# Two FP4 layers and the linear attention between them, chained: FP4's last and first turns placed among the linear tiles

## The chip, the cores and the metric

The kernel runs on one core of a Trainium2 chip. The core has four compute engines that each work through a queue of their own in order: TensorE (PE, with its weight loads shown apart as PEld), VectorE (DVE), ScalarE (ACT) and GpSimd (POOL), and a fifth, SyncE (SP), that issues DMAs. The metric is the device time of one execution in microseconds; the number compared is the median of several executions.

## The reference

Six layers work on `x` of 4 x 1024 tokens by 256 channels, each on the layer norm of `x`, each added back to it:

```
x = x + 0.5 * moe(norm(x))            # router over 4 experts, GELU
x = x + softmax_attention(norm(x))    # 16 heads, causal
x = x + 0.5 * moe(norm(x))
x = x + 0.5 * fp4_ffn(norm(x))        # first FP4 layer
x = x + linear_attention(norm(x))     # causal, 16 heads of 16
x = x + 0.5 * fp4_ffn(norm(x))        # second FP4 layer
```

The change concerns the last three. The FP4 layer is `fp4_linear(silu(gate) * up, w_down)` with `gate` and `up` each an `fp4_linear` of the input (256 to 704). `fp4_linear` first rounds both operands to a grid of sixteen signed values: per block of 16 elements `scale = max(max|x| / 6, 1e-12)`, then `q = nearest grid value of x / scale, times scale`. Both the layer's inputs and its hidden values (704 a token) go through it.

The linear attention takes `q`, `k`, `v` from one product of 256 to 768, passes `q` and `k` through `square(gamma * normalized + beta)`, and computes for each token `q . cumsum(k v^T)`, divided by `q . cumsum(k)`, and a last product of 256 to 256.

## The kernel before, in words

`x` lies in SBUF as eight tiles `x0` to `x7` of 128 partitions by 4 x 256 and stays there. Tokens are taken in 32 tiles of 128.

**An FP4 layer** (`fp4_phase`, L1122) runs sixteen turns, one for each pair of tiles, and two more that drain. All four engines have their order written out by hand here (`tc.manual_schedule`). One turn `p` works on several pairs at once:

- `fp4_statistics(p+3)` and `fp4_deviation(p+3)`: mean and variance on DVE (L1226, L1227), the root on ACT (L1232);
- `fp4_offset(p+2)`, `fp4_inputs(p+2)`: two tiny DVE operations (L1237, L1239) and the normalized input `xn` on ACT (L1247);
- `fp4_inputs_scale(p+2)`, `fp4_inputs_rounded(p+2)`: block maxima `xam`, their reciprocals, `xv = xn / scale`, the exponent `xm` (DVE, L1042 to L1051), `fp4_least` on ACT (L1057), two rounding operations on DVE (L1061, L1062) and `xq` on POOL (L1261);
- `fp4_inputs_turned(p+1)`: transposes of `xq` on PE (L1285), a copy on ACT;
- `fp4_products(p, j)` for both tiles `j` of the pair: eight matmul rows into `pairA` (gate) and eight into `pairB` (up) (L1298), then SiLU on ACT (L1307); `fp4_gated(p, j)` multiplies on DVE (L1312) into `h`;
- `fp4_scale` on both tiles' `h` at once: `ham`, `hrs`, `hv`, `hm` (the same lines L1042 to L1051, 128 x 1408), with the residual of `p-1` between the reciprocal and `hv`;
- in the next turn `fp4_hidden_begin` (two halves of `fp4_least` on ACT), `fp4_hidden_rounded(p-1, j)` (L1061, L1062 on DVE, `hq` on POOL, L1276), `fp4_hidden_turned(p-1, j)` (transposes L1319, copies L1320), `fp4_down` (L1327, into the one bank `acc`) and `fp4_residual` (L1334), which adds into `x`; in the last layer it also sends the tile out by a DMA on SP.

DVE's order at the start of a turn is: statistics of `p+3`, rounding of `p-1` tile 0, offset of `p+2`, rounding of `p-1` tile 1, gate of `p` tile 0.

**The linear attention** (`linear_phase`, L1342) works by single tiles. Only PE's order is written out; DVE, ACT and POOL are ordered by the framework's scheduler, which may also move such instructions ahead into the FP4 layer before. For a tile `n` there are: `linear_products(n)` (L1394; bias on DVE L1402, statistics L1407, root L1410 on ACT, normalized `qk` L1420, gamma and beta on POOL L1424, L1425, square on ACT into `ker`, L1427), `linear_turn` (transposes of `ker`, L1437, and four copies on ACT), `linear_scores` (L1456 into `pairA` and `pairB`, the causal mask on DVE into `sc`, L1465, the running state on PE, DVE and POOL, L1475 to L1498), `linear_values` (L1507 into `acc`), `linear_out` (L1522 to L1528), `linear_back` and `linear_project` (L1540, L1549, residual L1551). Step `n` runs scores of `n`, products of `n+2`, projection of `n-3`, turn of `n+1`, values of `n`, back of `n-2`, out of `n-1`. Every fourth tile `linear_inputs` normalizes a block of four (L263, L264, L281 on DVE, the bias into `x` on POOL, L1383) and transposes it (L290).

PSUM is divided into `pairA` and `pairB` of two banks each, `acc`, and three banks that all other products and transposes take in rotation (`bank`).

The three phases follow each other with their own pools: the linear pool opens where the first FP4 pool lay, the second FP4 pool where the linear one lay.

Of the kernel before, what the change touches and what calls it, by code (L numbers as in the profile page):

```python
# [21 lines left out]
P = 128  # L22
# [6 lines left out]
H = 16  # L29
# [17 lines left out]
def macaron_kernel(  # L47
# [985 lines left out]
    def fp4_scale(wp, src, n, parts, tag, pinned=lambda ins: ins, between=None):  # L1033

        def temp(name, shape):
            t = wp.tile([P] + shape, F32, tag=tag + name, name=tag + name)
            return t[0:parts]

        am = temp("am", [n])
        pinned(nc.vector.tensor_reduce(am, src, AX.X, ALU.max, apply_absolute_value=True))  # L1042
        nc.vector.tensor_scalar(am, am, SIXTH, 1e-12, ALU.mult, ALU.max)
        rs = temp("rs", [n])
        nc.vector.reciprocal(rs, am)
        if between:
            between()
        v = temp("v", [n, QB])
        nc.vector.tensor_tensor(v, src, rs.unsqueeze(2).to_broadcast([parts, n, QB]), ALU.mult)  # L1049
        m = temp("m", [n, QB])  # L1050
        nc.vector.tensor_scalar(m.bitcast(U32), v.bitcast(U32), 0x7F800000, None, ALU.bitwise_and)  # L1051
        return am, v, m
# [69 lines left out]
    def fp4_phase(tag, final, fetch=None, later={}):  # L1122
        np_ = TT // 2
        with tc.tile_pool(name=f"fp4{tag}", bufs=2, reuse_waits="tile") as wp, tc.manual_schedule(
            engines={mybir.EngineType.PE, mybir.EngineType.DVE, mybir.EngineType.Activation, mybir.EngineType.Pool}
        ):
            held = {}
            for p in range(5):
                fp4_fetch(wp, p, held, fetch)
            if fetch:  # L1130
                keep_awake(50)
                for p in range(2):
                    keep_awake(4, held["back", p][:, 1, 0:P])
            for p in range(2):
                fp4_returned(p, held)
                fp4_statistics(wp, p, held)
                fp4_deviation(wp, p, held)
            if fetch:
                keep_awake(12)
            for p in range(2):  # L1140
                fp4_offset(wp, p, held)
                fp4_inputs(wp, p, held)
            if fetch:
                keep_awake(4, held["xn", 0][:, 0:P])
                keep_awake(6)
            fp4_inputs_scale(wp, 0, held)
            fp4_inputs_rounded(wp, 0, held)
            fp4_inputs_turned(wp, 0, held)
            fp4_inputs_scale(wp, 1, held)
            fp4_returned(2, held)  # L1150
            fp4_statistics(wp, 2, held)
            fp4_inputs_rounded(wp, 1, held)
            fp4_deviation(wp, 2, held)
            fp4_returned(3, held)
            for p in range(np_ + 2):
                now, before = p < np_, 1 <= p <= np_
                if p in later:
                    later[p]()
                if before:
                    fp4_hidden_begin(wp, p - 1, held)  # L1160
                if p + 3 < np_:
                    fp4_statistics(wp, p + 3, held)
                if before:
                    fp4_hidden_rounded(p - 1, 0, held)
                if p + 2 < np_:
                    fp4_offset(wp, p + 2, held)
                if now:
                    fp4_products(wp, p, 0, held)
                if p + 2 < np_:
                    fp4_inputs(wp, p + 2, held)  # L1170
                if before:
                    fp4_hidden_rounded(p - 1, 1, held)
                if now:
                    fp4_gated(p, 0, held)
                if p >= 2:
                    fp4_down(wp, p - 2, 1, held)
                if p + 2 < np_:
                    fp4_inputs_scale(wp, p + 2, held)
                if p + 1 < np_:
                    fp4_inputs_turned(wp, p + 1, held)  # L1180
                if before:
                    fp4_hidden_turned(wp, p - 1, 0, held)
                if p >= 2:
                    fp4_residual(p - 2, 1, held, final)
                if p + 2 < np_:
                    fp4_inputs_rounded(wp, p + 2, held)
                if p + 4 < np_:
                    fp4_returned(p + 4, held, nc.gpsimd)
                if p + 5 < np_:
                    fp4_fetch(wp, p + 5, held, fetch)  # L1190
                if now:
                    fp4_products(wp, p, 1, held)
                    fp4_gated(p, 1, held)
                if p + 3 < np_:
                    fp4_deviation(wp, p + 3, held)
                if before:
                    fp4_down(wp, p - 1, 0, held)
                residual = (lambda: fp4_residual(p - 1, 0, held, final)) if before else None
                if now:
                    h = held.pop(("h", p))  # L1200
                    held["hs", p] = fp4_scale(
                        wp, blocks_of(h.rearrange("p j f -> p (j f)")), 2 * FI // QB, P, "h", between=residual
                    )
                elif before:
                    residual()
                if before:
                    fp4_hidden_turned(wp, p - 1, 1, held)
# [56 lines left out]
    def fp4_hidden_begin(wp, p, held):  # L1264
        am, v, m = held["hs", p]
        n = FI // QB
        for j in range(2):
            fp4_least(m[:, j * n : (j + 1) * n], P)
        held["hq", p] = wp.tile([P, 2, FI], F32, tag="hq", name="hq")

    def fp4_hidden_rounded(p, j, held):
        am, v, m = held["hs", p]
        n = FI // QB
        s = slice(j * n, (j + 1) * n)
        fp4_round(v[:, s], m[:, s])
        nc.gpsimd.tensor_tensor(  # L1276
            blocks_of(held["hq", p][:, j]), v[:, s], am[:, s].unsqueeze(2).to_broadcast([P, n, QB]), ALU.mult
# [64 lines left out]
    def linear_phase():  # L1342
        with tc.tile_pool(name="lin1", bufs=1, reuse_waits="tile") as cp, tc.tile_pool(
            name="lin", bufs=2, reuse_waits="tile"
        ) as wp, tc.manual_schedule(engines={mybir.EngineType.PE}):

            vas = [cp.tile([P, H, 32], F32, tag=f"va1{i}", name=f"va1{i}") for i in range(4)]


            state = cp.tile([P, KD, 8, 32], F32, tag="state", name="state")  # L1350
            for t in vas:
                nc.gpsimd.memset(t, 1.0)
            nc.gpsimd.memset(state, 0.0)
            held = {}

            def products(n):
                if n % TPB == 0:
                    linear_inputs(wp, n // TPB, held)
                linear_products(wp, n, vas[n % 4], held)

            for n in range(2):
                products(n)
            linear_turn(wp, 0, held)
# [278 lines left out]
```

## Time and profile before

| what | us |
|---|---|
| median of 3 runs (2437.53 to 2443.14) | 2441.64 |
| the profiled execution | 2446.59 |
| its span, first to last instruction | 2444.9 |
| first FP4 layer, its turns' `ham` from tile pair 0 to 15 | 1554.63 to 1822.40 |
| linear attention, first to last `sc` | 1863.67 to 2125.24 |
| second FP4 layer, `ham` of pair 0 to 15 | 2158.18 to 2420.45 |

Over the span PE is busy 2290.6 us (94%), DVE 1684.6 (69%), ACT 1006.1 (41%), POOL 726.1 (30%). These shares mix stages with different limits. A stage is read by asking the profile for the busy time of each engine in a stretch of the span; the granted clock is TensorE's, 1.00 being full speed. Matmuls are pipelined and their ends are modelled, so a busy PE is not PE at its peak. A steady FP4 turn takes 17.4 us, a linear tile 8.33 us (a tile with a block's transposes 9.9).

### The profile page before, as it was taken

The numbers are of one execution on the slowest core, as the hardware profiler recorded it, in microseconds if no ns is written. First come the engines' busy times: TensorE is split into PE (matmuls) and PEld (weight loads), VectorE is DVE, ScalarE is ACT, GpSimd is POOL, SyncE is SP. The second block draws the span as 40 slices with busy tenths as digits, with TensorE's granted clock in tenths as the row PEclk, the third lists the DMA queues.
The fourth block names the chain that finished last, engine by engine and source line by source line (L and its number), as shares of the span: only waits on it lengthen the run. The fifth ranks groups of instructions, "written<-read, shape, count | busy, mean of one in ns | idle before, by whom it ended". The sixth has DMA issues, their size and how long they took to land.

```text
span 2444.9 us, 37631 instructions
## 1 busy us (share of the span) xinstructions
PE 2290.6 (94%) x13607; PEld 1498.4 (61%) x13607; DVE 1684.6 (69%) x4625; ACT 1006.1 (41%) x2057; POOL 726.1 (30%) x816
## 2 busy tenths in 40 slices
PE   7999998999999999999989999899987999889998
PEld 5688884444344444444568887566765777656766
DVE  6456664766766777767533333899977888789996
ACT  3233332345544554553422332455533333345552
POOL 0344532121121111111144442455424443212221
PEclk7899999799999999998889999999998999989999
DMA  5333321011111111010043331010000000000000
GB/s 175 109 117 116 113 70 52 20 28 30 30 32 30 31 32 39 22 50 21 31 148 111 104 108 42 28 46 20 10 0 1 1 1 2 1 7 13 18 14 20
DMA packets 67554, 112.66 MB, mean 46 GB/s; under 512 B 20696, under 2 KB 47864, under 8 KB 62248
## 3 DMA queue, kind: packets, MB, share of 16 engines
q0 software_dynamic: 12192, 58.21, 7.4%
q1 hardware_dynamic: 53400, 47.44, 6.8%
q10 hardware_dynamic: 1776, 4.61, 0.6%
q8 instruction: 108, 1.77, 0.3%
q14 instruction: 78, 0.64, 0.1%
HBM read 74.11 MB, written 23.00 MB: 40 GB/s over the span
## 4 chain that ended last, share of the span: by engine, by line
PE 67%; DVE 22%; ACT 4%; issue 3%; POOL 3%; DMA 1%; another core or an unknown queue 0%; DVEq 0%; ACTq 0%; POOLq 0%; SPq 0%
PE acc L587 10%; PE bank L874 9%; PE bank L983 8%; PE acc L933 6%; PE pairA L571 6%; PE pairB L571 5%; PE bank L1394 3%; PE bank L829 3%; POOL hq L1276 2%; DVE ham L1042 2%; DVE h L1312 2%; DVE hv L1049 2%; PE bank L385 1%; PE bank L809 1%; PE bank L113 1%
## 5 line engine op out<-in xcount | busy, mean ns | idle before, releaser
L993 ACT ACTIVATE ex<-bank 128x512 f32<-128x512 f32 (+3 forms) x768 | 317.3, 497 | 352.6 <-PE bank L983 350.1
L996 POOL TENSOR_SCALAR_AFFINE_SELECT ex<-ex 128x256 f32<-128x256 f32 x256 | 103.9, 412 | 654.4 <-ACT ex L993 650.6
L874 PE MATMUL bank<-kT,qT 32*128 32x512 f32 (+3 forms) x1536 | 264.1, 551 | 6.6 <-ACT ex L993 5.5
L587 PE MATMUL acc<-wf,gT 128*128 128x256 f32 x1184 | 261.7, 379 | 0.0
L587 PEld LDWEIGHTS acc<-wf,gT 128*128 128x128 f32 x1184 | 225.0, 190 | 30.6
L593 DVE TENSOR_TENSOR y<-acc,xg 128x256 f32<-128x256 f32 x74 | 28.0, 419 | 294.9 <-issue 197.2
L983 PE MATMUL bank<-less,kT 32*128 32x512 f32 (+3 forms) x1536 | 216.0, 562 | 8.7 <-DVE mv L264 5.0
L887 DVE TENSOR_REDUCE part<-bank 128x1 f32<-128x512 f32 x256 | 160.3, 682 | 62.1 <-PE bank L874 61.6
L874 PEld LDWEIGHTS bank<-kT,qT 32*128 32x128 f32 x1536 | 120.2, 193 | 105.3 <-issue 41.8
L1327 PE MATMUL acc<-wdT,hqT 128*128 128x256 f32 x768 | 180.6, 386 | 3.4 <-DVE x L1334 2.8
L1276 POOL TENSOR_TENSOR hq<-hv,ham 128x704 f32<-128x704 f32 x64 | 106.8, 1669 | 256.5 <-DVE std L1237 154.0
L1298 PE MATMUL pairA<-wgT,xqT 128*128 128x352 f32 x512 | 169.0, 475 | 1.7 <-ACT xqT L1287 1.4
L1327 PEld LDWEIGHTS acc<-wdT,hqT 128*128 128x128 f32 x768 | 147.8, 193 | 35.6 <-ACT hqT L1320 4.0
L933 PE MATMUL acc<-ex,va 128*32 128x512 f32 (+3 forms) x1536 | 168.1, 513 | 0.1
L571 PE MATMUL pairA<-xgT,w 128*128 128x256 f32 x608 | 159.6, 385 | 8.9 <-ACT xgT L561 8.3
L983 PEld LDWEIGHTS bank<-less,kT 32*128 32x128 f32 x1536 | 81.5, 191 | 138.6 <-issue 88.4
L890 DVE CUSTOM_DVE_ANT_0 seen<-bank,mask_q,part 128x512 bf16<-128x512 f32 (+3 forms) x256 | 126.1, 547 | 54.5 <-PE bank L874 54.1
L1298 PE MATMUL pairB<-wuT,xqT 128*128 128x352 f32 x512 | 161.9, 459 | 0.0
L571 PE MATMUL pairB<-xgT,w 128*128 128x256 f32 x608 | 156.1, 379 | 0.0
L578 ACT ACTIVATE gT<-pairA,b1s 128x256 f32<-128x256 f32 x152 | 72.0, 473 | 167.7 <-PE pairA L571 163.8
L1298 PEld LDWEIGHTS pairB<-wuT,xqT 128*128 128x128 f32 x512 | 97.3, 190 | 54.3 <-issue 0.2
L890 DVE CUSTOM_DVE_ANT_0 seen<-bank,mask_q 128x512 bf16<-128x512 f32 (+3 forms) x256 | 111.2, 485 | 27.6 <-PE bank L874 24.8
(274 smaller groups left out, 4248.8 us busy)
## 6 DMA issues: line engine op xcount, KB each, us to landing
y_d<-y SPq DMA_DIRECT2D x36, 256.0 KB
xn_d<-xn SPq DMA_DIRECT2D x16, 512.0 KB
x<-in_x SPq DMA_DIRECT2D x8, 512.0 KB
kT<-qk SPq DMA_DIRECT2D x32, 128.0 KB
qT<-qk SPq DMA_DIRECT2D x32, 128.0 KB
yT<-ys SPq DMA_DIRECT2D x32, 128.0 KB
out<-x SPq DMA_DIRECT2D x32, 128.0 KB
den<-inv_d SPq DMA_DIRECT2D x112, 32.0 KB
```

The lines of the kernel that those rows point to most:

```text
L571: nc.tensor.matmul(pg[:, f, :], lhsT=w1[:, k * FF + fc * P : k * FF + (fc + 1) * P], rhs=xgT[:, k, :], start=(k == 0), stop=(k == KD - 1),)
L587: nc.tensor.matmul(po[j], lhsT=gT[fc][:, bass.ts(j, P)], rhs=wf0[:, fc, :], start=(fc == 0), stop=(fc == NF - 1))
L874: nc.tensor.matmul(ps[:, 0:cols], lhsT=qT[rows, bass.ts(qt, P)], rhs=kT[rows, c * BLK : c * BLK + cols], start=True, stop=True,)
L887: nc.vector.tensor_reduce(parts[i][:, h : h + 1], ps[:, 0:cols], AX.X, ALU.max, negate=True)
L890: nc.vector.tensor_tensor_reduce(out=seen[:, 0:cols], in0=ps[:, 0:cols], in1=mask_q[:, BLK - cols : BLK], scale=-1.0, scalar=parts[i][:, h ...
L933: nc.tensor.matmul(acc[qb][bass.ts(h, 32), c0:BLK], lhsT=va[:, kt, NG * g + h, :], rhs=exs[h // 2][:, h % 2, c0:BLK], start=(kt == 0), sto ...
L983: nc.tensor.matmul(pss[h][:, c0:BLK], lhsT=kT[rows, bass.ts(kt, P)], rhs=held["less", n, qb][rows, c0:BLK], start=True, stop=True,)
L993: nc.scalar.activation(ex[:, j, c0:BLK], pss[2 * a + j][:, c0:BLK], AF.Exp, scale=0.25)
L996: nc.gpsimd.affine_select(out=ex[:, :, c0 : c0 + P], in_=ex[:, :, c0 : c0 + P], compare_op=ALU.is_ge, fill=0.0, base=0, pattern=[[0, 2], [ ...
L1276: nc.gpsimd.tensor_tensor(blocks_of(held["hq", p][:, j]), v[:, s], am[:, s].unsqueeze(2).to_broadcast([P, n, QB]), ALU.mult)
L1298: nc.tensor.matmul(pg[:, half, 0:FIH], lhsT=held["xqT", p][:, k, j, :], rhs=w[:, k, half * FIH : (half + 1) * FIH], start=(k == 0), stop=( ...
L1327: nc.tensor.matmul(po, lhsT=hqT[:, c, :], rhs=wdT[:, c, :], start=(c == 0), stop=(c == NFI - 1))
```

## The change

The three phases become one function, `fp4_and_linear`, with all pools open at once. What it does:

1. **The order within an FP4 turn.** `fp4_phase` is split into `fp4_begin` and a generator `fp4_turn`. The statistics of `p+3` move behind the first rounding, the offset of `p+2` ahead of it; the residual of `p-1` moves from between `hrs` and `hv` to behind `hm`. In the first and the last turn (`apart`) the hidden scale is done in two halves, the first one, with its rounding, before the second gate.
2. **Linear within the last FP4 turns.** Turn 14 holds the norm of block 0, turn 15 the transposes and products of linear tile 0, and the products of tile 1 follow it; the order is written out for all engines.
3. **FP4's two draining turns** become steps behind `linear_values` of tiles 0 to 2 (1, 2 and 4 steps).
4. **The second FP4 layer's beginning** (`fp4_first`, six steps, and its turns 0 to 2, eleven steps) is placed one step a tile behind `linear_values` of tiles 20 to 31 and of the three draining steps; the last steps follow the loop. On PE they stand where they are written; on DVE, ACT and POOL `behind()` holds them back behind the last instruction that each of these queues had when the step was written.
5. **The norms** of linear blocks 1 to 7 become such steps too, at every fourth tile, two tiles ahead of their transposes; the linear `xn` takes its room from the FP4 tag `hq`, and the scores `sc` become two tiles in the rooms of `hv` and `hm` (two buffers each, as `sc` had).
6. The memsets of `va1` and `state` on POOL (L1352, L1353) move ahead of the first FP4 layer.

The diff, cut to its core:

```diff
-    def fp4_phase(tag, final, fetch=None, later={}):
...
+    def fp4_turn(wp, p, held, final, fetch=None):
         np_ = TT // 2
+        now, before = p < np_, 1 <= p <= np_
+        if before and p - 1 not in (0, np_ - 1):
+            for j in range(2):
+                fp4_hidden_least(p - 1, j, held)
+        if p + 2 < np_:
+            fp4_offset(wp, p + 2, held)
+        if before and p - 1 not in (0, np_ - 1):
+            fp4_hidden_rounded(p - 1, 0, held)
+        if p + 3 < np_:
+            fp4_statistics(wp, p + 3, held)
+        if now:
+            fp4_products(wp, p, 0, held)
+        if p + 2 < np_:
+            fp4_inputs(wp, p + 2, held)
+        if before:
+            fp4_hidden_rounded(p - 1, 1, held)
+        if now:
+            fp4_gated(p, 0, held)
+        if p >= 2:
+            fp4_down(wp, p - 2, 1, held)
+        yield
...
+        apart = p in (0, np_ - 1)
+        if now:
+            fp4_hidden_begin(wp, p, held)
+            fp4_products(wp, p, 1, held)
+        if now and apart:
+            fp4_hidden_scale(p, 0, 1, held)
+            fp4_hidden_least(p, 0, held)
+            fp4_hidden_rounded(p, 0, held)
+        if now:
+            fp4_gated(p, 1, held)
...
+        if now and not apart:
+            fp4_hidden_scale(p, 0, 2, held)
+        if before:
+            fp4_residual(p - 1, 0, held, final)
+        if now and apart:
+            fp4_hidden_scale(p, 1, 1, held)
+            fp4_hidden_least(p, 1, held)
...
+        yield
+        if before:
+            fp4_hidden_turned(wp, p - 1, 1, held)
+            yield
...
+    @contextmanager
+    def behind():
+        traced = nc.cur_bb.bb.instructions
+        with ExitStack() as stack:
+            for engine in (mybir.EngineType.DVE, mybir.EngineType.Activation, mybir.EngineType.Pool):
+                stack.enter_context(tc.issue_after(next(i for i in reversed(traced) if i.engine == engine)))
+            yield
...
+            with tc.manual_schedule(engines=all_four):
+                fp4_begin(wp, held, fetch)
+                for p in range(np_):
+                    if p in later:
+                        later[p]()
+                    turn = fp4_turn(wp, p, held, False, fetch)
+                    next(turn)
+                    if p == np_ - 2:
+                        linear_norm(wp, 0, lin)
+                    if p == np_ - 1:
+                        linear_inputs(lp, 0, lin)
+                        linear_products(lp, 0, vas[0], lin)
+                    for _ in turn:
+                        pass
+                linear_products(lp, 1, vas[1], lin)
+            ends = itertools.chain(*(fp4_turn(wp, p, held, False) for p in (np_, np_ + 1)))
             held = {}
...
+            first = itertools.chain(fp4_first(wp, held), *(fp4_turn(wp, p, held, True) for p in range(3)))
+            with tc.manual_schedule(engines={mybir.EngineType.PE}):
+                linear_phase(lp, wp, vas, state, ends, first, lin)
+            with tc.manual_schedule(engines=all_four):
+                for p in range(3, np_ + 2):
+                    for _ in fp4_turn(wp, p, held, True):
+                        pass
...
+        step_behind(ends)
+        linear_turn(wp, 0, held)
+        for n in range(TT + 3):
...
+            if n < TT:
+                linear_values(wp, n, vas[n % 4], held)
+            for _ in range((1, 2, 4)[n] if n < 3 else 0):
+                step_behind(ends)
...
+            if n >= TT - 12:
+                step_behind(first)
+            if n % TPB == 0 and n + TPB < TT:
+                with behind():
+                    linear_norm(fwp, n // TPB + 1, held)
+            if 2 <= n < TT + 2:
+                linear_back(wp, n - 2, held)
+            if 1 <= n < TT + 1:
+                linear_out(wp, n - 1, held)
...
+    def linear_norm(fwp, b, held):
+        xn = fwp.tile([P, 2, FI], F32, tag="hq", name="hq").rearrange("p j f -> p (j f)")
+        xn = xn[:, 0 : TPB * D].rearrange("p (i d) -> p i d", d=D)
         norm_block(xn, xb[b], eps5)
         nc.gpsimd.tensor_tensor(xb[b], xb[b], over_tiles(bo1), ALU.add)
+        held["xn", b] = xn
...
-        sc = wp.tile([P, 4, KD, 2, P], F32, tag="sc", name="sc")
-        for a in range(2):
+        sc = []
+        for a, tag in enumerate(("hv", "hm")):
+            room = fwp.tile([P, 2, FI // QB, QB], F32, tag=tag, name=tag).rearrange("p j n c -> p (j n c)")
+            sc.append(room[:, 0 : 8 * P].rearrange("p (r g e t) -> p r g e t", r=2, g=KD, e=2))
```

## The prediction

> **What bounds the kernel now.** I read the table by stages first, then the instructions of one steady FP4 turn, then those of one linear tile, then the two seams and the tail. All the change's work lies behind 1554 us of the span.
>
> Stages (columns: stretch, its length, then busy us of PE, PEld, DVE, ACT, POOL, granted clock, DMA share, GB/s):
>
> ```profile
> 1747.21:1786.89 39.68, 35.54 (x157) 26.00 (x157) 38.27 (x89) 24.51 (x37) 9.28 (x8) 1.00 0.00 0
> 1805.48:1863.67 58.19, 41.63 (x174) 29.19 (x173) 41.37 (x85) 15.32 (x30) 21.16 (x16) 0.87 0.00 1
> 1896.52:2033.30 136.78, 134.96 (x1321) 100.52 (x1321) 115.59 (x286) 51.86 (x136) 59.14 (x50) 1.00 0.01 1
> 2033.30:2211.91 178.61, 159.15 (x1202) 116.12 (x1203) 144.29 (x309) 76.32 (x157) 48.12 (x42) 0.94 0.01 4
> 2211.91:2386.62 174.71, 166.17 (x722) 122.75 (x721) 163.77 (x257) 96.49 (x148) 45.89 (x31) 1.00 0.05 16
> 2420.45:2444.90 24.45, 14.52 (x61) 11.30 (x60) 10.95 (x13) 4.33 (x8) 3.26 (x2) 0.86 0.07 22
> ```
>
> Rows 1 and 5 are FP4 turns: DVE is busy 94 to 96%. Row 3 is the steady linear phase: PE 99%, DVE 85%. Rows 2 and 4 hold the seams FP4 to linear and linear to FP4, and row 6 the end: there nothing is full and the granted clock falls to 0.86.
>
> One steady turn, 17.47 us from `ham` to `ham`, DVE and POOL rows:
>
> ```profile
> 2217.16 0.42 DVE L1226 BATCH_NORM_STATS2 st<-x 128x6 f32<-128x256 f32 x1
> ...
> 2218.24 0.86 DVE L1061 SCALAR_TENSOR_TENSOR hv<-hm,hv 128x704 f32<-128x704 f32 x1
> 2219.13 0.89 DVE L1062 SCALAR_TENSOR_TENSOR hv<-hm,hv 128x704 f32<-128x704 f32 x1
> ...
> 2220.21 0.88 DVE L1061 SCALAR_TENSOR_TENSOR hv<-hm,hv 128x704 f32<-128x704 f32 x1
> 2221.13 1.96 DVE L1062 SCALAR_TENSOR_TENSOR hv<-hm,hv 128x704 f32<-128x704 f32 x1
> 2223.01 0.88 DVE L1312 TENSOR_TENSOR h<-pairB,h 128x704 f32<-128x704 f32 x1
> ```
> ```profile
> 2185.07 1.39 POOL L1276 TENSOR_TENSOR hq<-hv,ham 128x704 f32<-128x704 f32 x1 [9.05 <-DVE std L1237]
> 2220.19 2.15 POOL L1276 TENSOR_TENSOR hq<-hv,ham 128x704 f32<-128x704 f32 x1 [7.96 <-DVE std L1237]
> ```
>
> The last rounding takes 1.96 instead of 0.89 us and ends 0.75 us after POOL's `hq`: DVE and POOL take turns here. So the turn is DVE's own chain, and "busy" holds 1.07 us of waiting.
>
> One linear tile (8.33 us) and the last tile's scores:
>
> ```profile
> 1966.05 1.21 DVE L1465 TENSOR_TENSOR sc<-pairB,keep_kq 128x1024 f32<-128x1024 f32 x1
> 1968.18 0.69 DVE L1402 TENSOR_TENSOR qk<-bank,bqkv 128x512 f32<-128x512 f32 x1 [0.57 <-PE bank L1394]
> 1969.71 0.60 PE L1437 MATMUL bank<-ident,ker 128*128 128x128 f32 x4
> 1970.24 1.08 PE L1507 MATMUL acc<-sc,va 128*32 128x128 f32 x32
> 2142.83 1.12 PE L1285 MATMUL bank<-ident,xq 128*128 128x128 f32 x4 [9.48 <-POOL xq L1261]
> ```
>
> PE needs `sc` 3 us after it is ready, and the bank that `qk` frees at 1968.87 0.84 us later: that is the slack a later DVE has. The last row is the seam: PE idle 9.48 us until FP4's first input is rounded.
>
> **The change part by part.** Zero is the profiled execution, 2446.59 us (span 2444.9 and 1.69 around it), 4.95 us above the median 2441.64. I take differences from the trace to the median.
>
> *A, order within a turn.* `fp4_residual` (0.28 on the chain) goes from before `hv` to behind `hm`, the statistics (four instructions, 2217.16 to 2218.24, 1.08) from before the first rounding to between the two. Then `hv` starts 0.20 earlier, `hm` ends at 2217.04, and ACT's first `fp4_least` half (1.66/2 = 0.83, with 0.07 of hand-offs) lets the rounding start at 2217.94: 0.30 earlier. Residual (0.36) and offset (0.3) end before that, so ACT is what is late next. From first rounding to the gate: now 4.77. Afterwards two roundings end at 1.78, POOL starts 0.17 later (2220.02 to 2220.19), and from POOL's start to the gate I use the turn in which POOL came first (2185.07 to 2188.05), 2.98: together 4.93, 0.16 more. Net −0.14 a turn; 11 turns of the first layer and 10 of the second have this form: −2.9. Bounds: the whole 1.07 saved, −22; or ACT's bare 0.95 wait (the turns without statistics show it) not covered, +6.
>
> *B, linear statistics leave FP4 turns.* Turns 11 and 12 take 20.13 and 19.55 us against 17.40 because 20 of linear's `L263` statistics ran inside them: −4.9. They return in D.
>
> *C, FP4 into linear.* Before, from `ham` of turn 14 (1805.48) to the first `sc` (1863.67) 58.2 us. After, in DVE's new order from that `ham`: to the end of `hm` 5.1, waits and roundings of tile pair 14 5.4, gate 0.9, linear's `qk` chain of tile 0 3.9, residual 0.4, half a hidden scale (0.82+0.18+0.37+0.82+0.45) 2.65: 18.4. The rounding behind it needs `fp4_least`, which on ACT queues behind `ker` of tile 0, which waits for POOL's gamma and beta: 15.4+2.6+0.63 `ker`, two `hqT` copies 0.86, table load 1.28, silu 0.76, least 0.83: 22.4. So here the new wait costs 4. Then rounding 1.7, gate 0.9, residual 0.4, half scale 2.65, `qk` chain of tile 1 3.9, rounding 1.7: first `sc` at 33.7, 24.5 earlier. PE's share (two products 5.2, `xn` transposes 0.9 in the turn) lies in its 4.35 us wait for `hq` and in DVE's 33.7. What is left of layer one, two `hqT` transposes 1.3 and two downs 5.2, now lies between linear tiles, where PE is full: +6 of PE, no cover. C = −18.5. Bounds: all of that hidden, −26; the ACT/POOL queueing met a second time and a third, −8. The five memsets (0.53 each) now go ahead of the ten `back` gathers on POOL's queue; POOL is idle 14.49 us there, so nothing; without that cover, 2.6.
>
> *D, linear's norms inside linear.* Each block puts statistics (2.2) and `xn` (1.77) between `yn` and `sc` of one tile. DVE is then 3.3 late after 0.6 of idle time; 0.57 (idle before `qk`) and 0.84 (bank slack) absorb some, PE waits 1.9, less the 0.7 that tile 4k+2 now waits (9.90 us against 8.33+0.86). +1.2 for each of the four blocks between: +4.6. Bounds −3 (stalls vanish) and +16 (nothing absorbed). POOL's bias add (2.38) now stands ahead of the `state` add, which has 6 us until its reader.
>
> *E, the second layer behind linear.* Before, from `sc` of tile 20 (2033.30) to `ham` of turn 3 (2211.91) 178.6. After: tiles 20 to 25 are DVE's: 40.7 busy, 4.4 statistics, 11.2 for FP4's first inputs, 3 of waits: 59 instead of 50. Tiles 26 to 34 and the rest of turn 2: I take per step the larger of PE (8.33 a tile, 4.76 per product pair, 2.6 per down) and DVE (7.0 a tile and the turn's pieces): 13.9, 10.7, 14.9, 13.1, 7.5, 12.7, 2.4, 9.8, 4.5, 8.0 = 97.5, and 2 for the gate that waits behind `ker` on ACT at tile 28. To `ham` 3: 12.2. Sum 170.7: −7.9. Bounds: PE's work alone at full clock, 155, −24; a wait of 1.3 in each of 14 steps, +10. I stay near the larger-of sum since both engines are 90% full.
>
> [...]
>
> *F, the end.* Before, `ham` 14 to the end is 41.4. The halved last scale runs in DVE's 3.9 us wait for pair B: gate at 10.5, half scale to 14.4, least 15.3, rounding 17.0, gate, residual, second half 20.9, least and rounding 23.5, POOL 25.1, transposes behind `down` 27.2, last down 29.9, residual 30.3, and the same 3.9 to the end: 34.2, −7.1 (−9 if PE is free earlier, −4 if the clock stays low). Output DMAs keep number and order.
>
> Sum: −2.9 −4.9 −18.5 +4.6 −7.9 −7.1 = −36.7, so 2404.9.
>
> **Rivals.** *Better fill:* E reaches PE's 155 and the ACT wait in C vanishes: 16 and 4 more, 2385. For it: DVE has 149 of work there. Against: in-order queues with hand-offs. *Seams keep their waits:* C −8 and E +4 (each step waits): −14, 2427. For it: ACT serves silu, square and least in one queue. *Slower:* DVE's lag reaches PE in every linear tile, at the bank in front of the `ker` transposes, where the slack is 0.84. Without D the gains are 41.3; over 32 tiles that is 1.29 us a tile, 1.44 to be measurably slower (0.2%, 4.9 us, is what a measurement of this kernel can tell from no change). At 2 us a tile: +23, 2464. For it: 85% DVE before the norms are added. Against: only one tile in four gets 4 us. *The overlap does not happen* (queues end up serial): A, B and F alone, but the moved PE work of C and D's norms on the path (+6, +4.6): about 2437, inside 0.2%.
>
> **How the numbers follow.** Forecast 0.52 (its own range 2388 to 2420), better fill 0.18, kept waits 0.15, no change 0.03, slower 0.12. Faster is 0.52+0.18+0.15 = 0.85. The range reaches into the better fill (2378, between its 2385 and the sum of lower bounds) and past the kept waits (2434); it leaves out the slower case and some of the best one.
>
> **What would show it.** `hq` of a steady turn takes 1.39 throughout, a turn 17.3; turns 11 and 12 like the others; first `sc` 34 us after `ham` 14; linear blocks of 35 us instead of 34; no stretch with a clock under 0.9 around either seam; from tile 20 to `ham` 3 about 171; the tail 10 us after the last gate. Wrong if the `ker` transposes on PE wait for DVE's `qk` in each tile, if ACT's `ker` holds up the gates by more than 4 us, or if DVE waits for released `hv`/`hm` space.

## The result, and the profile after

The changed kernel takes 2458.91 us in the median of four runs (2453.82 to 2465.04), the kernel before 2442.39; the ratio is 1.0068, 95% interval 1.0043 to 1.0092. It is about 16.6 us slower, where 2405 was forecast.

The profiled execution after took 2453.82 us, the lowest of its four, 7.2 above the profiled one before. The difference is larger in the part that the change concerns: up to the first returned tile that DVE adds to `x` (L1219 before, L1293 after) the two executions took 1529.14 and 1520.99 us for the same work (1515 to 1531 over all fourteen kernels profiled), and from there to the end 915.76 and 931.11: +15.35. So I compare stretches from there on. "Hidden maximum" is the first `ham` instruction of a turn on 128 x 1408 elements, "scores" the first masking instruction of a linear tile.

| stretch (us) | before | after | difference | term, forecast |
|---|---|---|---|---|
| first returned tile to hidden maximum 1 | 43.8 | 44.5 | +0.7 | |
| hidden maximum 1 to 13 | 214.0 | 208.5 | -5.5 | A and B, -1.5 -4.9 |
| 13 to 14 | 18.6 | 18.3 | -0.3 | |
| 14 to scores of tile 0 | 58.2 | 40.4 | -17.8 | C, -24.5 |
| scores of tile 0 to 4 | 32.9 | 46.6 | +13.7 | C, +6 |
| tile 4 to 20 | 136.8 | 151.9 | +15.1 | D, +4.6 |
| tile 20 to hidden maximum 3 of the second layer | 178.6 | 190.4 | +11.8 | E, -7.9 |
| hidden maximum 3 to 14 | 191.6 | 191.1 | -0.5 | A, -1.4 |
| 14 to the end | 41.4 | 39.6 | -1.8 | F, -7.1 |

The table by stages after, with the columns as before (stretch, length, busy us of PE, PEld, DVE, ACT, POOL, granted clock, DMA share, GB/s):

```profile
1792.28:1832.64 40.36, 32.11 (x135) 22.61 (x134) 29.39 (x49) 15.10 (x25) 12.11 (x8) 0.88 0.00 1
1832.64:1879.22 46.58, 39.22 (x345) 28.56 (x345) 29.86 (x78) 13.52 (x36) 13.49 (x12) 0.95 0.01 1
1879.22:2031.10 151.88, 139.23 (x1321) 102.26 (x1321) 119.30 (x323) 52.63 (x140) 58.64 (x49) 0.98 0.01 1
2031.10:2221.47 190.37, 167.78 (x1206) 119.36 (x1207) 150.25 (x340) 78.68 (x161) 54.11 (x44) 0.96 0.01 4
2221.47:2395.79 174.32, 167.48 (x718) 121.07 (x717) 160.49 (x256) 95.63 (x148) 38.83 (x31) 1.00 0.05 16
2412.55:2452.10 39.55, 30.87 (x129) 23.31 (x128) 22.68 (x31) 9.01 (x16) 6.04 (x4) 0.90 0.06 20
```

Row 3 is the surprise: the steady linear phase, 99% PE before, is now 92% PE at a clock of 0.98, and DVE is only 79% busy. Neither engine is full: both wait.

**D, a norm in the linear phase.** `add` is the instruction with which DVE takes a tile's own part of the running state out of its bank. The waits of tiles 4 to 20 (engine, what waited, for whom, us in total, times, longest): PE's only one before, then PE's largest after, and DVE's for the norm's root:

```profile
PE bank L1394 <- DVE add L1496: 1.8, 4, 0.5
```
```profile
PE bank L1653 <- DVE add L1600: 10.8, 4, 2.8
DVE rstd L271 <- ACT std L270: 7.9, 4, 2.0
```

One of these four in order of time:

```profile
1925.82 0.42 DVE L1632 TENSOR_TENSOR yn<-bank,den 128x256 f32<-128x256 f32 x1
1926.06 1.27 POOL L1527 TENSOR_TENSOR qk<-qk,bet 128x512 f32<-128x512 f32 x1
1927.36 0.63 ACT L1529 ACTIVATE ker<-qk 128x512 f32<-128x512 f32 x1 [2.32 <-POOL qk L1527]
1927.89 0.28 ACT L270 ACTIVATE std<-mv,eps 128x4 f32<-128x4 f32 x1
1928.21 0.18 DVE L271 RECIPROCAL rstd<-std 128x4 f32<-128x4 f32 x1 [1.97 <-ACT std L270]
1928.42 1.38 DVE L281 TENSOR_SCALAR hq<-x,mv,rstd 128x256 f32<-128x256 f32 x4
```

The norm's statistics were done at 1925.6, but its root stands on ACT behind `ker`, and `ker` waits for POOL's gamma and beta. DVE, in order, stands still for 1.97 us; the scores, and `add` behind them, come that much later, and PE's projection (L1653) waits 2.8 us for the bank that `add` reads. With two smaller waits of 0.9 in total each PE stands 12.6 us in tiles 4 to 20, 10.8 more than before. Two of the four tiles with the long wait also ran at a lower clock, 0.81 for 1.00, and took 3.2 us more (last section). Waits and clock together make 14.0 of the +15.1.

**A, a steady turn.** DVE's rows from the residual's new place to the gate, then POOL's of the same turn:

```profile
2226.57 0.42 DVE L1417 SCALAR_TENSOR_TENSOR x<-acc,x 128x256 f32<-128x256 f32 x1
...
2227.61 0.89 DVE L1058 SCALAR_TENSOR_TENSOR hv<-hm,hv 128x704 f32<-128x704 f32 x1 [0.35 <-ACT hm L1054]
...
2230.42 1.30 DVE L1058 SCALAR_TENSOR_TENSOR hv<-hm,hv 128x704 f32<-128x704 f32 x1
2231.76 0.89 DVE L1059 SCALAR_TENSOR_TENSOR hv<-hm,hv 128x704 f32<-128x704 f32 x1
2232.57 0.88 DVE L1395 TENSOR_TENSOR h<-pairB,h 128x704 f32<-128x704 f32 x1
```
```profile
2229.59 1.39 POOL L1359 TENSOR_TENSOR hq<-hv,ham 128x704 f32<-128x704 f32 x1 [7.80 <-DVE hv L1059]
2232.73 1.39 POOL L1359 TENSOR_TENSOR hq<-hv,ham 128x704 f32<-128x704 f32 x1 [1.75 <-DVE hv L1059]
```

`hq` takes 1.39 both times and the 1.96 row is gone, as forecast. The first rounding starts 6.14 us after the hidden maximum, for 6.33 before: 0.19 earlier, where 0.30 was forecast. From there to the gate it is 4.96 us instead of 4.77 (forecast 4.93): the second rounding, 1.30 long, meets POOL's first `hq`, and from POOL's start to the gate it is 2.98 us, as forecast; the statistics, now between the two roundings, lie in that time. So from hidden maximum to gate it is 11.10 us (2221.47 to 2232.57), as before (2211.91 to 2223.01).

**C, the first seam.** From pair 14 to tile 1, PE and ACT:

```profile
1821.13 2.08 PE L1496 MATMUL bank<-wqkv,xnT 128*128 128x256 f32 x4 [4.53 <-DVE qk L1504]
1823.00 4.53 PE L1410 MATMUL acc<-wdT,hqT 128*128 128x256 f32 x12
...
1828.76 0.63 ACT L1529 ACTIVATE ker<-qk 128x512 f32<-128x512 f32 x1 [5.01 <-POOL qk L1527]
1829.29 0.35 ACT L1541 COPY fkT<-bank 128x256 f32<-128x256 f32 x1
...
1830.44 0.80 PE L1558 MATMUL pairA<-fqT,fkT 32*128 32x256 f32 x2 [2.47 <-ACT fqT L1544]
...
1841.26 0.42 PE L1611 MATMUL acc<-hv,va 128*32 128x128 f32 x8 [2.90 <-DVE x L1417]
```

DVE's chain ends about where I had it (its last rounding at 1827.6, 35.3 us after the hidden maximum, for 33.7). But tile 0's `ker`, ready at 1810.9, is transposed on PE only behind the products of tile 1, which wait 4.53 us for DVE's `qk`, and behind a `down` that takes 4.53 us, at a granted clock of 0.60, instead of some 2.8 (1827.4). Its copies `fkT`, `fqT` then stand on ACT behind the `ker` of tile 1, 1.3 us more. The last row is the price of the drain among the tiles: linear's values and FP4's `down` share the bank `acc`, and PE waits for a residual that DVE does only behind the next tile's chain.

**E, the second seam.** From the scores of tile 26 to those of tile 27, 18.5 us:

```profile
2100.50 5.46 PE L1496 MATMUL bank<-wqkv,xnT 128*128 128x512 f32 x8 [2.99 <-DVE add L1600]
2104.36 0.69 DVE L1504 TENSOR_TENSOR qk<-bank,bqkv 128x512 f32<-128x512 f32 x1 [4.01 <-PE bank L1496]
2111.71 0.63 ACT L1529 ACTIVATE ker<-qk 128x512 f32<-128x512 f32 x1 [1.18 <-POOL qk L1527]
2114.44 0.89 DVE L1395 TENSOR_TENSOR h<-pairB,h 128x704 f32<-128x704 f32 x1 [4.97 <-ACT h L1390]
2114.46 0.70 PE L1558 MATMUL pairA<-fqT,fkT 32*128 32x256 f32 x4 [0.28 <-ACT h L1390]
```
```profile
2097.67:2116.17 18.50, 15.16 (x86) 9.72 (x86) 8.62 (x25) 8.51 (x16) 4.31 (x4) 0.82 0.00 0
```

There is one chain through all engines: PE waits for `add`, DVE for PE's products, POOL for DVE, `ker` for POOL, FP4's silu for `ker`, and the next scores for the silu, which frees `pairA`. DVE is busy for less than half of the stretch (8.62 us). PE is busy for 15.16, since FP4's products stand beside the chain, but at a granted clock of 0.82.

**F, the end.** ACT, PE and POOL behind the second half of the last hidden scale:

```profile
2434.29 0.88 ACT L1054 ACTIVATE hm<-hm,halves 128x704 f32<-128x704 f32 x1 [5.98 <-DVE hm L1049]
2435.08 0.84 ACT L1403 COPY hqT<-bank 128x384 f32<-128x384 f32 x2
2435.59 5.49 PE L1410 MATMUL acc<-wdT,hqT 128*128 128x256 f32 x12 [4.13 <-ACT hqT L1403]
2437.10 1.39 POOL L1359 TENSOR_TENSOR hq<-hv,ham 128x704 f32<-128x704 f32 x1 [5.38 <-DVE hv L1059]
2442.05 2.86 PE L1410 MATMUL acc<-wdT,hqT 128*128 128x256 f32 x12 [0.29 <-ACT hqT L1403]
2445.86 2.86 PE L1410 MATMUL acc<-wdT,hqT 128*128 128x256 f32 x12 [0.30 <-ACT hqT L1403]
```

The last `hq` starts 24.6 us after hidden maximum 14 (and ends at 25.9, for a forecast of 25.1). But three `down` have then still to end, one after another through the one bank: the first waited 4.13 for a copy that stands on ACT behind a `least` which waits for DVE, and takes 5.49, at a granted clock of 0.51, instead of 2.86, at 1.00; the other two are 3.8 apart.

### The profile page after: what moved, and what is told of

It reads as the page before. It is cut to its first block, busy times and chain, and to the rows that moved or that the text cites. A ratio compares the mean times of both kernels' runs of the same rounds, so it can differ in the third digit from the quotient of the medians.

```text
span 2452.1 us, 37599 instructions
## 1 busy us (share of the span) xinstructions
PE 2294.8 (94%) x13607; PEld 1494.8 (61%) x13607; DVE 1675.2 (68%) x4645; ACT 1005.3 (41%) x2059; POOL 713.7 (29%) x816
## 4 chain that ended last, share of the span: by engine, by line
PE 63%; DVE 22%; ACT 7%; issue 4%; POOL 2%; DMA 2%; another core or an unknown queue 0%; DVEq 0%; ACTq 0%; POOLq 0%; SPq 0%
PE acc L587 10%; PE bank L874 9%; PE bank L983 8%; PE acc L933 6%; PE pairA L571 6%; PE pairB L571 5%; PE bank L829 3%; PE bank L1496 2%; DVE h L1395 2%; DVE hv L1048 2%; DVE ham L1045 2%; PE bank L385 1%; PE bank L809 1%; PE acc L1410 1%; ACT hm L1054 1%
## 5 line engine op out<-in xcount | busy, mean ns | idle before, releaser
L1410 PEld LDWEIGHTS acc<-wdT,hqT 128*128 128x128 f32 x768 | 146.6, 194 | 46.6 <-issue 14.4
L1359 POOL TENSOR_TENSOR hq<-hv,ham 128x704 f32<-128x704 f32 x64 | 91.7, 1433 | 258.6 <-DVE hv L1059 258.6
L1381 PE MATMUL pairA<-wgT,xqT 128*128 128x352 f32 x512 | 163.8, 463 | 1.4 <-ACT h L1390 0.7
L571 PEld LDWEIGHTS pairA<-xgT,w 128*128 128x128 f32 x608 | 106.6, 189 | 37.0 <-ACT xgT L561 14.6
```

What stands on the lines that cost most here:

```text
L571: nc.tensor.matmul(pg[:, f, :], lhsT=w1[:, k * FF + fc * P : k * FF + (fc + 1) * P], rhs=xgT[:, k, :], start=(k == 0), stop=(k == KD - 1),)
L1359: nc.gpsimd.tensor_tensor(blocks_of(held["hq", p][:, j]), v, am.unsqueeze(2).to_broadcast([P, n, QB]), ALU.mult)
L1381: nc.tensor.matmul(pg[:, half, 0:FIH], lhsT=held["xqT", p][:, k, j, :], rhs=w[:, k, half * FIH : (half + 1) * FIH], start=(k == 0), stop=( ...
L1410: nc.tensor.matmul(po, lhsT=hqT[:, c, :], rhs=wdT[:, c, :], start=(c == 0), stop=(c == NFI - 1))
```

## The experiments

What was expected of each run stands ahead of its account; "theory" and "rival" are meant as named there. All in one table, the stretches as above (us). "Whole" is the ratio to the kernel before with its interval, "start to end" runs from the first returned tile to the end in the profiled execution. A stretch that an edit leaves alone repeats well (hidden maximum 1 to 13 takes 208.4 to 208.5 in all eleven variants of the changed kernel; 14 to the end, at a granted clock of 0.90 in the changed kernel, 38.4 to 39.9), so the stretches tell more than the whole. A stretch in which tiles with a PE wait ran at a lower granted clock (0.81 and 0.66, last section) does vary: tiles 4 to 20 take 151.6 to 154.7 in the five kernels with the norm as changed.

| run | whole | start to end | 14 to scores 0 | 0 to 4 | 4 to 20 | 20 to maximum 3 | 14 to end |
|---|---|---|---|---|---|---|---|
| before | 1 | 915.8 | 58.2 | 32.9 | 136.8 | 178.6 | 41.4 |
| changed | 1.0068 (1.0043, 1.0092) | 931.1 | 40.4 | 46.6 | 151.9 | 190.4 | 39.6 |
| order_only | 0.9978 (0.9958, 0.9998) | 912.2 | 57.2 | 32.8 | 136.8 | 178.7 | 38.7 |
| norm_split | 1.0024 (1.0006, 1.0042) | 920.9 | 40.3 | 45.8 | 149.3 | 184.5 | 38.6 |
| norm_spread | 0.9995 (0.9979, 1.0011) | 914.3 | 40.4 | 46.6 | 142.1 | 184.4 | 38.6 |
| no_first | 1.0051 (1.0028, 1.0073) | 931.4 | 40.4 | 46.6 | 154.7 | 187.7 | 39.8 |
| silu_first | 1.0058 (1.0036, 1.0080) | 927.9 | 40.4 | 46.6 | 154.7 | 184.7 | 39.3 |
| ends_before | 1.0040 (1.0011, 1.0070) | 924.4 | 46.9 | 34.9 | 151.6 | 189.5 | 39.6 |
| ends_bank | 1.0070 (1.0043, 1.0098) | 927.8 | 40.4 | 42.9 | 153.2 | 189.7 | 39.4 |
| spread_ends_nofirst | 0.9974 (0.9958, 0.9991) | 908.4 | 46.9 | 35.0 | 142.0 | 183.8 | 38.4 |
| spread_ends_late | 0.9958 (0.9944, 0.9972) | 903.5 | 46.9 | 34.9 | 142.0 | 177.6 | 39.9 |
| best4 | 0.9942 (0.9919, 0.9965) | 896.7 | 46.9 | 35.7 | 136.7 | 175.3 | 39.9 |
| best6 | 0.9917 (0.9896, 0.9938) | 893.6 | 46.9 | 37.5 | 136.7 | 170.7 | 39.5 |
| best8 | 0.9907 (0.9889, 0.9924) | 891.4 | 46.9 | 35.8 | 136.7 | 171.2 | 38.6 |

### A and F alone

```diff
             for p in range(np_ + 2):
                 if p in later:
                     later[p]()
-                if before:
-                    fp4_hidden_begin(wp, p - 1, held)
...
+                for _ in fp4_turn(wp, p, held, final, fetch):
+                    pass
```

> The kernel before with the new order of an FP4 turn and the halved scale in the first and the last turn, nothing else. The prediction's terms A and F: -2.9 and -7.1, 2432. What the two traces show: a turn of 17.41 and 17.47 as before (0), the first turn +0.7, the end -1.8: 2441, the same as before.

Between the two: 0.22% faster (5 us). Hidden maximum 3 to 14 is 191.1 for 191.6, but a steady turn takes 17.47 us as before: the 0.5 is in the last two turns of that stretch (12 to 13 17.04 for 17.46, 13 to 14 16.77 for 16.92). The end is -2.7; the turns 1 to 13, which keep linear's statistics here, -0.8, and 13 to 14 of the first layer -1.8. The first turn, with its scale in two halves, lost 3.2 (not pursued).

### D: the norm in two pieces, in three, and in three cut otherwise

`norm_split`:

```diff
             if n % TPB == 0 and n + TPB < TT:
                 with behind():
-                    linear_norm(fwp, n // TPB + 1, held)
+                    linear_norm_begin(n // TPB + 1, held)    # statistics, root
+            if n % TPB == 1 and n + TPB < TT:
+                with behind():
+                    linear_norm_end(fwp, n // TPB + 1, held)  # 1/std, xn, bias
```

> The changed kernel with each linear norm cut in two: statistics and root behind the values of tile 4k, reciprocal, xn and bias behind those of tile 4k+1. Theory Q (place in the queue): in the changed kernel the root stands on ACT behind ker of two tiles on, DVE waits for it in order (1.97 us), and PE then waits 2.8 us a block for the bank that add frees. Then the wait of DVE for the root and that of PE vanish, tiles 4 to 20 take about 140 us instead of 151.9, and the whole 2445 (-12 to -15 against 2458.9). Theory V (volume): the 4 us of DVE work alone make the lag; halved, each half still loses 0.4 to 0.8 beyond the 1.4 that a tile absorbs: tiles 4 to 20 about 146, the whole 2452. The prediction's own price (1.2 a block) would leave nothing to gain: 2457.

The wait for the root is gone, as theory Q has it, and yet tiles 4 to 20 take 149.3. In the second tile of a block (DVE, POOL and the wait of PE):

```profile
1967.01 3.03 DVE L1504 TENSOR_SCALAR hq<-x,mv,rstd 128x256 f32<-128x256 f32 x3
1967.23 1.30 POOL L1552 TENSOR_TENSOR qk<-qk,gam 128x512 f32<-128x512 f32 x1 [3.21 <-DVE qk L1548]
1968.62 1.27 POOL L1553 TENSOR_TENSOR qk<-qk,bet 128x512 f32<-128x512 f32 x1
1973.61 2.82 PE L1522 MATMUL bank<-wqkv,xnT 128*128 128x512 f32 x8 [1.98 <-DVE add L1626]
```

An `xn` alone takes 0.41 (the first of the four, at 1966.03); three beside POOL's gamma and beta take 3.03 instead of 3 x 0.41 and end 0.15 us after POOL does; over tiles 4 to 20 an `xn` takes 0.90 in the mean, 0.41 in the changed kernel. There the wait for the root had kept `xn` clear of POOL (the four from 1928.42 to 1929.80, POOL's beta done at 1927.33, its next row from 1929.88), so taking the wait away put this in its place: 1.8 us a block. And the late scores now fall on the tile with the block's transposes, where the products themselves need the bank of `add`: there PE already waits 0.45 us in the kernel before.

`norm_spread`:

```diff
...
+            if n >= 2 and n % TPB != 1:
+                ahead, part = (n + 6) // TPB, (n + 6) % TPB
+                if ahead * TPB < TT:
+                    with behind():
+                        linear_norm_part(fwp, ahead, part, held)
...
+        if part < 2:
+            for i in range(2 * part, 2 * part + 2):   # statistics; root with part 1
...
+        if part == 2:                                 # 1/std, xn of four tiles, bias
```

> The changed kernel with the norm of each linear block from 2 on cut in three, none of them at a tile 4k+1: two tiles' statistics behind the values of tile 4k+2, two and the root at 4k+3, reciprocal, xn and bias at 4k+4. Theory B (bank): PE waits for the bank that add reads; in an ordinary tile that bank has 1.2 us to spare, in the tile that follows 4k+1, whose transposes take two banks more, none. Then pieces of 1.1, 1.1 and 1.6 cost nearly nothing: tiles 4 to 20 in 138 to 140 us (the changed kernel 151.9, the norm in two 149.3, the kernel before 136.8), the whole about 2442. Theory V (volume: DVE has no room for 4 us a block, wherever they stand): 146 to 149, the whole about 2449.

142.1: theory V falls, theory B holds but for 1.3 us a block. The tiles with statistics are no longer than before; the excess is in the tile of `xn` (10.6 instead of 8.3, of which the next makes up 1.1), where three `xn` take 3.03 again. The whole is level with the kernel before. `best4` (below) cuts the same work once more, so that no more than two `xn` stand in a tile; they take 0.41 each, ahead of gamma or around the normalization of `qk`, and what PE waits for in tiles 4 to 20 is what it waited for before the change:

```profile
PE bank L1524 <- DVE add L1628: 1.8, 4, 0.5
```

136.7 us: the norm costs nothing here. Of its 4 us a block the kernel before had 2 among these tiles as well (`xn`; its statistics ran in FP4 turns and at the first seam), so what is free is the other 2, and another place for the rest. The same instructions cost 15.1 us in the changed kernel: DVE's volume was not the limit.

### E: the second layer's steps left out of the loop, or its silu put first

`no_first`:

```diff
-            if n >= TT - 12:
-                step_behind(first)
```

> The changed kernel with the steps of the second FP4 layer all behind the linear loop instead of one a tile from tile 20 on. From the scores of tile 20 to the hidden maximum of turn 3 the changed kernel takes 190.4, the kernel before 178.6. Theory S (steps cost more than they hide): serial again it takes 178.6 plus two norms of 4: 186.6, the whole 2455; if the steps are all of the loss, 178.6 and 2447. Rival G (the overlap does gain its 8, the two norms and the FP4 drain eat it): it grows by 8 or more, 198, the whole 2467 or more.

Tile 20 to hidden maximum 3 takes 187.7 for 190.4: near theory S (186.6), and two norms account for it: tiles 20 to 26 take 57.5 for 50.2 before, tiles 26 to 31 40.6 as before. So the steps as placed cost 2.7 us more than they hide. (Tiles 4 to 20 took 2.8 longer here, by one more tile at a lower clock, 0.66: last section.)

`silu_first`:

```diff
             if n + 2 < TT:
                 products(n + 2)
+                if n not in (26, 28, 29):
+                    linear_square(wp, n + 2, held)       # ker
...
             if n >= TT - 12:
                 step_behind(first)
+            if n in (26, 28, 29):
+                with tc.issue_after(second["silu"]):
+                    linear_square(wp, n + 2, held)
```

> The changed kernel with the linear ker of tiles 28, 30 and 31 held on ACT behind the silu of the second FP4 layer's first products instead of ahead of it. Theory L (the silu queued behind ker is what makes these tiles slow: DVE waits 7.4 us for it in two places, PE 2.2): tiles 26 to 31 go from 71.0 to 65 or less, tile 20 to the hidden maximum of turn 3 from 190.4 to 185, the whole 2453. Rival: every step chains the four engines once more, and another wait takes its place: within 1.5 us of 190.4, the whole 2458.

184.7, and tiles 26 to 31 65.3 for 71.0: theory L, by the stretch. DVE's 7.4 us of waits for the silu are gone (a wait of 3.8 for `pairB` has come). The whole doesn't show it: tiles 4 to 20 lost 2.8 as above, and the interval is wider than the rest.

### C: the drain in front, or in banks of its own

`ends_before`:

```diff
                 linear_products(lp, 1, vas[1], lin)
-            ends = itertools.chain(*(fp4_turn(wp, p, held, False) for p in (np_, np_ + 1)))
+                for p in (np_, np_ + 1):
+                    for _ in fp4_turn(wp, p, held, False):
+                        pass
...
```

> The changed kernel with the first FP4 layer's two draining turns ahead of the first linear scores instead of between tiles 0 to 2. From the hidden maximum of turn 14 to the scores of tile 0 the changed kernel takes 40.4, from there to tile 4 46.6 (before: 58.2 and 32.9). Theory: the draining steps are what makes the first tiles slow: first scores 7 to 10 later (48 to 50), tiles 0 to 4 down to 37 (32.9 and one norm of 4), sum 86 and the whole 2458, the same. Rival: norm and waits of linear itself make the first tiles slow: they stay at 44 to 46 and the whole is 5 to 8 slower, 2465.

First scores 6.5 later, tiles 0 to 4 11.7 shorter: the drain among the tiles costs 5.2 more than it hides. The theory had the two even.

`ends_bank`:

```diff
-        po = acc_bank([P, D])
+        po = bank([P, D]) if held.get("own") else acc_bank([P, D])
...
+            held["own"] = True
             ends = itertools.chain(*(fp4_turn(wp, p, held, False) for p in (np_, np_ + 1)))
```

> The changed kernel with the down products of the two draining turns in the rotating banks instead of the one bank acc that linear's values use too. Theory A (shared bank: in tiles 0 to 2 PE waits 2.9 for the residual that frees acc, 2.5 and 0.6 for the copy yt, and DVE 5.1 for the down products): tiles 0 to 4 go from 46.6 to about 41. Rival (in-order chains of DVE and ACT: the residual stands behind the next tile's chain in any bank): within 1.5 us of 46.6.

42.9, two thirds of theory A's gain: the shared bank is 3.7 us of the 11.7. PE's waits for residual and `yt` are gone; one of 2.9 for the bank of `add` is there in their place. What the other 8 are was not run down.

### What is left when each part is placed where it is free

`spread_ends_nofirst` joins `norm_spread`, `ends_before` and `no_first`; `spread_ends_late` starts the second layer's steps at tile 28 instead:

```diff
-            if n >= TT - 12:
+            if n >= TT - 4:
                 step_behind(first)
```

> Norm in three pieces, the first FP4 layer's draining turns ahead of the first linear scores, and the second layer's steps from tile 28 on instead of 20. From parts measured so far: first scores 46.9 after the hidden maximum of turn 14, tiles 0 to 4 34.9, 4 to 20 139, 20 to 31 92. Theory: where tiles 30 to 34 have no products left, the steps hide behind PE: scores of tile 31 to the hidden maximum of turn 3 from 87.8 (before) to 75, the whole 27 below the kernel before: 2413. Rival: the steps cost in the last tiles what they save behind them: 87, the whole 2425.

> As the run before, with the second layer's steps all behind the linear loop. By the sum of parts (44.3, 208.4, 18.3, 46.9, 34.9, 139, 179.5, 191.1, 39.6) 902 from the first returned tile to the end, 14 below the kernel before: 2426. If the run before gains nothing by its late steps, the two are alike.

The late steps save 6.2 us between tile 20 and hidden maximum 3 (177.6 for 183.8): 2.1 more in tiles 26 to 31, 8.3 less behind. From the scores of tile 31 to hidden maximum 3 it is 82.0, for 87.8 before; the theory asked 75. The whole falls short of 2413 for other reasons too: tiles 4 to 20 take 142.0 for 139, 20 to 31 95.5 for 92.

`best4` is the same with statistics and root at tile 4k+2 and two `xn` each at 4k+3 and 4k+4; `best6` and `best8` start the steps at tile 26 and 24.

> Draining turns ahead of the first scores, the second layer's steps from tile 28 on, and the norm in three pieces of another cut: all statistics and the root behind the values of tile 4k+2, two tiles' xn at 4k+3, two and the bias at 4k+4. With the whole xn in one tile (measured before) tiles 4 to 20 took 142.0, all of its excess in the tile of xn (10.6 instead of 8.3). If a tile's spare 1.2 us is what counts, two xn (0.9) are free and four statistics with the root (2.2) cost 0.4 a block: 138.5, the whole 4 to 6 below 2433.9: 2429. If each block costs 1.3 however it is cut: 142 and 2434.

> The same with the second layer's steps from tile 26 on instead of 28. From 28 on they saved 8.3 us behind the last scores for 2.1 in tiles 26 to 31. Two steps more: if the last tiles still have room, 3 us less than from tile 28 on; if tiles 26 to 29, whose products keep DVE full, take them at full price, the same within 1.5 us.

> As the run before, with the second layer's steps from tile 24 on instead of 26: its first silu then stands in step 30, the first one in which no linear product and no ker is left. Theory S (what made the changed kernel's steps dear are the norms and the silu beside ker, not the steps themselves): 2 to 4 more in tiles 24 to 31, 6 less behind them: from tile 20 to the hidden maximum of turn 3 167 against 170.7, the whole 2417. Theory V (DVE and PE are both full in tiles 24 to 29, each step costs there what it saves later): 170 to 172, the whole as from tile 26 on.

`best4` gains 6.7 us from start to end, as if a tile's spare time is what counts; `best6` 3 more (section 893.6 for 896.7; 4.6 in its own stretch, less 1.7 in tiles 2 to 4 that the edit does not touch). The stretch from tile 20 to hidden maximum 3 in `best6`:

```profile
2023.60:2194.28 170.68, 158.95 (x1206) 116.15 (x1207) 147.29 (x330) 76.10 (x158) 53.35 (x45) 0.98 0.01 4
```

Nearly the same instructions as in row 4 of the changed kernel (10 of DVE's 340 fewer), in 19.7 us less: PE is busy 159 us instead of 168 for the same 1206, at a clock of 0.98 instead of 0.96, and idle 11.7 instead of 22.6. `best8` is no shorter there (171.2): from tile 24 on, a step costs what it saves, as theory V says. `best6` and `best8` beat both kernels, by 0.8% and 0.9%, about 20 to 23 us.

## Why the prediction was wrong

Sum and profile differ by 52 us behind the first returned tile: 19.7 in E, 14.4 in C, 10.5 in D, 5.3 in F, the rest in A and the first turn. In the first three the step that failed is of one kind: work set beside other work was priced by the time of PE and DVE that it takes, while its place in the queues, behind something that itself waits, was left out or had as a bound alone.

- **A** -2.9: nothing in a steady turn, 17.47 us before and 17.48 after; -0.6 in turns 13 and 14 of the second layer. The mechanism was right, DVE's and POOL's order too (4.96 us from first rounding to gate, for 4.93). What was mis-sized is the start of the first rounding, 0.30 earlier by the sum and 0.19 measured, and that 0.11 is most of the 0.14 a turn.
- **B** -4.9: right. Turns 11 and 12 are like the others (17.4 and 17.0 for 20.05 and 19.63); the stretch with both A and B gave -5.5.
- **C** -18.5: it was -4.1. Of the 14.4, 6.7 are first scores at 40.4 and not 33.7. The sum ended with DVE's last rounding, which came at 35.3, and took PE's share as covered by it; but PE only then turned tile 0's `ker`, behind products and a `down`, and ACT's copies, scores and mask follow. ACT's queue itself, which I had as a bound, is 1.3 of it. Another 5.7 is the drain, 11.7 for "+6 of PE": 3.7 go with the bank that `down` shares with the values (`ends_bank`), the rest is open. The last 2.0 stay in `ends_before` (34.9 for 32.9), with the norm of block 1 among those tiles, for which no term had a price.
- **D** +4.6: it was +15.1, just inside the bound of +16. The slack was looked for at the wrong bank. I took the 0.84 of the bank that `qk` frees; PE waited at the one that `add` frees, with 1.2 us to spare in an ordinary tile and none in a block's first tile (both before the change; `add` ends at 1941.07):

```profile
1940.64 0.43 DVE L1496 TENSOR_TENSOR add<-bank,own 128x272 f32<-128x272 f32 x1
1942.30 1.03 PE L1549 MATMUL bank<-wo,yT 128*128 128x256 f32 x4
1949.54 2.82 PE L1394 MATMUL bank<-wqkv,xnT 128*128 128x512 f32 x8 [0.45 <-DVE add L1496]
```

Beside it was what I did not price: the root's place behind `ker`, 2 us of a DVE that stands still, and 3.2 us more in the two tiles at a clock of 0.81. The rival "slower" had PE waiting on a late DVE, but in every tile, at the wrong bank, for want of DVE time; `best4`, with the same DVE work at no cost, refutes that last part.
- **E** -7.9: it was +11.8, beyond its bound of +10. By its own pieces: tiles 20 to 26 took 66.6 for 59, 26 to 31 71.0 for 62, the rest 52.8 for 49.6. "The larger of PE and DVE" per step holds only where neither waits for the other within the step; the tiles with silu are tied by one chain through four queues. I had 2 us, once, for a gate behind `ker`; DVE waited 4.97 and 2.4. DVE rows that grow longer beside POOL's, as by 1.07 us in a steady turn before, are a small part at most: DVE is busy 150 us where 149 were counted. Of the 19.7 too many, `silu_first` took back 5.7 and a cut norm 6; both together were not run, and 1.7 of each lie in the same place (52.8 to 51.1 behind the scores of tile 31), so they may not add up. The 8 or more that this would leave are open; that steps ahead of tile 26 save nothing (`best8` against `best6`) speaks for the full tiles in which they stand. That 170.7 was reached in `best6` with other places for the same steps is chance and does not make the sum right: it counted the steps of tiles 20 to 25 as hidden.
- **F** -7.1: it was -1.8 (-2.7 by itself). The last `hq` came 0.8 us later than I said; I counted one `down` behind it where PE had two to do and a third still running at a clock of 0.51.

Of the rivals, "seams keep their waits" came nearest in kind, for its reason too (ACT serves silu, square and least in one queue), but with C -8 and E +4 its 2427 is still 32 us short. One of the signs of being wrong came as written: ACT's `ker` held up a gate by more than 4 us (4.97).

## What to carry to other kernels

Work that is moved beside other work has to be priced at its place in each in-order queue: who stands ahead of it there, what that one waits for, and how much later each buffer it holds can come free. Busy shares, even per step, say only what could fit. If a step proves dear, cut it and try its places one by one against the length of the stretch: the same norm cost 3.8, 3.1, 1.3 and 0 us a block here, by its places alone.

## What the runs showed of the hardware

A PE wait of 2.6 to 2.8 us cost more than its length in some tiles here, and not always the same. Four tiles of the changed kernel hold such a wait and the same PE work; two of them, both with a wait of 2.6:

```profile
1891.49:1900.35 8.86, 6.27 (x64) 4.46 (x63) 6.76 (x18) 2.54 (x8) 5.59 (x4) 0.81 0.00 0
1969.04:1976.28 7.24, 4.64 (x64) 3.45 (x63) 6.75 (x18) 2.32 (x7) 4.10 (x3) 1.00 0.01 2
```

At a granted clock of 0.81 the tile takes 8.86 us, at 1.00 7.24; the two with a wait of 2.8 differ in the same way (8.82 at 0.81, 7.24 at 1.00). In `no_first` and `silu_first` one more tile met it, at 0.66, and took 10.1: that is their 2.8 us between tiles 4 and 20. After the 2.99 us wait behind the scores of tile 26 eight products took 5.46 instead of 2.74, at 0.50. Of the four tiles with waits of 2.6 to 2.8 us, two ran at 0.81 and two at 1.00; what decides between them no run here shows.
